# A graph layer's row gathers: two units in 60 fetched row by row from the queues of SyncE and ScalarE

## The chip, the core and the metric

The kernel runs on one core of a Trainium2 chip. A core has TensorE (PE in the profile; PEld is its loading of weights), VectorE (DVE), ScalarE (ACT), GpSimd (POOL) and SyncE (SP). They run side by side, each through its own instructions in order, and wait for each other through semaphores. SP, ACT and POOL can each start DMAs. The metric is the time of one execution on the device, in microseconds.

## What is computed

There are 50,000 nodes with 160 numbers each (64 scalars and 32 vectors of three), and 1,650,000 edges, sorted by their target `dst`. Each edge has four numbers, `sh`. The reference, cut to what matters:

```python
ss, vv = s[src], v[src]                      # 64 scalars, 32 vectors of the source node
e0, e1 = sh[:, 0:1], sh[:, 1:4]
dot = jnp.einsum('eui,ei->eu', vv, e1)
out0 = C0 * (ss * e0 @ W1 + dot * INV3 @ W2)
p3 = (ss @ W3)[:, :, None] * e1[:, None, :] * INV3
p4 = jnp.einsum('eui,uw->ewi', vv * e0[:, :, None], W4) * INV3
p5 = jnp.einsum('eui,uw->ewi', jnp.cross(vv, e1[:, None, :]), W5) * INV6
out1 = C1 * (p3 + p4 + p5)
m_agg = segment_sum(concatenate([out0, out1]), dst, num_segments=n)
h = m_agg's scalars @ Ws * LIN_S, m_agg's vectors by Wv * LIN_V
y = x + (x + relu(h))
out = (y - mean) / sqrt(var + 1e-5)          # over the 160 numbers of a node
```

All of it is linear in the source row times one of four edge numbers. The kernel therefore sums those products by target first and applies the weights, folded into one matrix for each edge number, after the sum. What is left for each edge is to fetch a row of 640 bytes.

## The kernel before

**Tiles.** A *unit* is 128 edges, one on each partition. Six units (`G`) make a *group*, whose edges have targets within a window of 32 nodes (`W`). Two groups (`PG`) make a *pair* of 12 units, and 20 groups (`SG`) a *section* of 120 units. There are 2,149 groups, 1,075 pairs and 108 sections, all written out by Python loops.

**Loading a section.** `load` (L186) runs one section ahead. SP fetches the section's source and target indices (`ri`) and edge numbers (`ra`), 120 units by 128. ACT casts the indices to `rf`, PE transposes them so that a unit becomes a column, and DVE casts the sources back to integers (`si`). The edge numbers stay transposed in PSUM as `pk`. `place` (L208) subtracts each group's first target (`rel`).

**A pair.** `group_sums` (L219) has POOL issue one indirect DMA for each unit (L225). It takes 128 row addresses from a column of `si` and writes 128 rows of `x` into `xg`, of which pool `rowp` has eight buffers. DVE compares targets with slot numbers (`hot`, L230) and multiplies by the four edge numbers (`ha`, L233). For each unit PE multiplies `ha` with `xg` (L238) into `ps` (two buffers), and ACT copies `ps` to `A` (L241).

**Two pairs.** `apply_weights` (L244) transposes `A` on PE (`pt`, L253), copies it on ACT to two tiles `at` (L256), multiplies with the folded weights (`phc`, L263) and copies the result on ACT to `hp` (L267). `block` (L270) sums the windows into blocks of 128 nodes with a 0/1 matrix (`phb`, L286). The node's own rows come by a DMA on SP (`xt`, L275) and are doubled on ACT (`x2`, L277). `norm` (L143) adds and normalizes on DVE, with a square root on ACT (`rstd`, L152), and ACT's queue writes the rows out (L156).

**Order.** The loop calls `group_sums` of a pair before the weights of the two pairs ahead of it. The order on each engine is then made by a scheduler when the program is built. It also deals the DMAs of SP and ACT over eight completion semaphores: a DMA waits until the one that used its semaphore before has landed.

**Later passes.** L358 and on handle indices that don't fit the windows. A flag is loaded into registers (L359). For these inputs their loops run zero times.

Of the kernel before, what the change touches and what calls it, by code (L numbers as in the profile page):

```python
# [29 lines left out]

F32 = mybir.dt.float32
I32 = mybir.dt.int32
AF = mybir.ActivationFunctionType
ALU = mybir.AluOpType
AX = mybir.AxisListType
ET = mybir.EngineType
PSUM = bass.MemoryType.PSUM

P = 128
MUL0, MUL1 = 64, 32  # L40
D = MUL0 + 3 * MUL1
# [10 lines left out]
QG = P // W  # L52
PG = 2
SG = 20


def plan(n_nodes, n_edges):

    nblk = 125
    assert n_nodes % nblk == 0  # L60
    nb = n_nodes // nblk
    again = 9

    per_unit = P * n_nodes / n_edges
    group = max(g for g in range(1, 17)
                if g == 1 or g * per_unit + 1 + 5 * math.sqrt(g * per_unit * per_unit / P) <= W)
    ngroups = math.ceil(math.ceil(n_edges / P) / group)
    units = P * math.ceil(max(math.ceil(n_edges / P) + again - 1, QG * math.ceil(ngroups / QG) * group) / P)
    return nblk, nb, again, group, units, ngroups
# [3 lines left out]
def tile_gnn_resnorm(ctx: ExitStack, tc: tile.TileContext, x, src, dst, attr, W1, W2, W3, W4, W5, Ws, Wv, out, n_edges):  # L73
    nc = tc.nc
    N = x.shape[0]
    NBLK, NB, GA, G, NU, NG = plan(N, n_edges)
# [14 lines left out]
    BWb = const.tile([D - P, NK, D], F32, name="BWb")  # L91
    more = const.tile([1, 2], I32, name="more")

    src1 = src.rearrange("(e o) -> e o", o=1)
    dst1 = dst.rearrange("(e o) -> e o", o=1)

    def weights(wp, psum):
# [45 lines left out]
    def norm(pool, ph, x2, n, row):  # L143
# [7 lines left out]
        rstd = pool.tile([P, 1], F32, name="rstd")  # L151
        nc.scalar.activation(rstd[:n], mv[:n, 1:2], AF.Sqrt, bias=eps_t[:n])  # L152
        nc.vector.reciprocal(rstd[:n], rstd[:n])  # L153
# [15 lines left out]
    alive = max(bs[-1] - bs[0] for bs in of_block) + 1  # L169
    NSC = math.ceil(NG / SG)  # L170

    with tc.tile_pool(name="once", bufs=1) as once, tc.tile_pool(name="raw", bufs=2) as rawp, \
            tc.tile_pool(name="idx", bufs=2) as idxp, tc.tile_pool(name="rows", bufs=8) as rowp, \
            tc.tile_pool(name="ops", bufs=3) as op, tc.tile_pool(name="sums", bufs=4) as sump, \
            tc.tile_pool(name="hp", bufs=alive + 3) as hpp, tc.tile_pool(name="node", bufs=3) as np_, \
            tc.tile_pool(name="psC", bufs=1, space=PSUM) as psC, tc.tile_pool(name="psK", bufs=2, space=PSUM) as psK, \
# [9 lines left out]
        def load(s):  # L186

            n = (min(NG, (s + 1) * SG) - s * SG) * G
            u0 = s * SG * G
            e = slice(u0 * P, (u0 + n) * P)  # L190
            ri = rawp.tile([P, 2, P], I32, name="ri")
            ra = rawp.tile([P, P, NK], F32, name="ra")
            nc.sync.dma_start(ri[:n, 0, :], src1[e].rearrange("(u p) o -> u (p o)", p=P))
            nc.sync.dma_start(ri[:n, 1, :], dst1[e].rearrange("(u p) o -> u (p o)", p=P))
            nc.sync.dma_start(ra[:n].rearrange("u p k -> u (p k)"), attr[e].rearrange("(u p) k -> u (p k)", p=P))
            rf = rawp.tile([P, 2, P], F32, name="rf")
            nc.scalar.copy(rf[:n], ri[:n])
            pi = psI.tile([P, 2, P], F32, name="pi")
            for i in range(2):
                nc.tensor.transpose(pi[:, i, :n], rf[:n, i, :], ident[:n, :n])  # L200
            si = idxp.tile([P, P], I32, name="si")
            nc.vector.tensor_copy(si[:, :n], pi[:, 0, :n])  # L202
            pk = psK.tile([P, NK, P], F32, name="pk")
            for k in range(NK):
                nc.tensor.transpose(pk[:, k, :n], ra[:n, :, k], ident[:n, :n])
            return s, n, si, pi, pk

        def place(loaded):  # L208

            s, n, si, pi, pk = loaded  # L210
            rel = idxp.tile([P, P], F32, name="rel")
            nc.vector.tensor_tensor(
                rel[:, :n].rearrange("p (g j) -> p g j", j=G), pi[:, 1, :n].rearrange("p (g j) -> p g j", j=G),
                baseB[:, s * SG:s * SG + n // G].unsqueeze(2).to_broadcast([P, n // G, G]), op=ALU.subtract)
            nc.vector.tensor_reduce(extremes[:, 0, s:s + 1], rel[:, :n], axis=AX.X, op=ALU.min)
            nc.vector.tensor_reduce(extremes[:, 1, s:s + 1], rel[:, :n], axis=AX.X, op=ALU.max)
            return si, rel, pk

        def group_sums(placed, u, ng):  # L219

            si, rel, pk = placed
            n = ng * G
            xg = rowp.tile([P, PG * G, D], F32, name="xg")
            for j in range(n):
                nc.gpsimd.indirect_dma_start(  # L225
                    out=xg[:, j, :], out_offset=None, in_=x,
                    in_offset=bass.IndirectOffsetOnAxis(ap=si[:, u + j:u + j + 1], axis=0))

            hot = op.tile([P, PG * G, W], F32, name="hot")
            nc.vector.tensor_tensor(hot[:, :n], slotsP[:, 0:W].unsqueeze(1).to_broadcast([P, n, W]),  # L230
                                    rel[:, u:u + n].unsqueeze(2).to_broadcast([P, n, W]), op=ALU.is_equal)
            ha = op.tile([P, PG * G, NK, W], F32, name="ha")
            nc.vector.tensor_tensor(ha[:, :n], hot[:, :n].unsqueeze(2).to_broadcast([P, n, NK, W]),  # L233
                                    pk[:, :, u:u + n].rearrange("p k u -> p u k").unsqueeze(3)
                                    .to_broadcast([P, n, NK, W]), op=ALU.mult)
            ps = psA.tile([P, PG, D], F32, name="ps")
            for j in range(n):
                nc.tensor.matmul(ps[:, j // G, :], ha[:, j].rearrange("p k w -> p (k w)"), xg[:, j, :],  # L238
                                 start=j % G == 0, stop=j % G == G - 1)
            A = sump.tile([P, PG, D], F32, name="A")  # L240
            nc.scalar.copy(A[:, :ng], ps[:, :ng])  # L241
            return A, ng

        def apply_weights(pairs):  # L244
# [3 lines left out]
            for f0, f1 in ((0, P), (P, D)):  # L248
                pt = psM.tile([P, QG, P], F32, name="pt", tag="misc")
                g = 0  # L250
                for A, n in pairs:
                    for i in range(n):
                        nc.tensor.transpose(pt[:f1 - f0, g, :], A[:, i, f0:f1], ident)  # L253
                        g += 1
# [15 lines left out]
        def block(b, hps):  # L270
# [15 lines left out]
                nc.tensor.matmul(ph[:nb], hot2[:r, i, :nb], hp[:r], start=i == 0, stop=i == len(cs) - 1)  # L286
            norm(np_, ph[:nb], x2[:nb], nb, row)

        loaded = {0: load(0)}


        base_d = dram.tile([NGP, 1], I32, name="base_d")
        with nc.allow_non_contiguous_dma(reason="one number of each group"):
            nc.sync.dma_start(base_d, dst1[0:NGP * G * P].rearrange("(g e) o -> g (e o)", e=G * P)[:, 0:1])
        baseI = once.tile([P, NGP], I32, name="baseI")
        nc.sync.dma_start(baseI, base_d.rearrange("g o -> o g").to_broadcast([P, NGP]))
# [3 lines left out]
        for g in range(QG):  # L300
            r = slice(g * W, (g + 1) * W)
# [4 lines left out]
        placed = {0: place(loaded.pop(0))}  # L306
# [10 lines left out]
        g = 0  # L317
        while g < NG:
            s = g // SG
            if g % SG == 0 and s + 1 < NSC:  # L320
                loaded[s + 1] = load(s + 1)
            ng = min(PG, NG - g, (s + 1) * SG - g)
            got = group_sums(placed[s], (g - s * SG) * G, ng)
            if ready:
                second(*ready.pop())
            pairs.append(got)
            g += ng
            if g % QG == 0 or g == NG:
                ready.append((c, pairs))
                pairs, c = [], c + 1  # L330
            if g % SG == 0 and g < NG:
                placed[s + 1] = place(loaded.pop(s + 1))
                del placed[s]
# [3 lines left out]
        far = once.tile([P, NCH], F32, name="far")  # L337
# [25 lines left out]
    mm_d = dram.tile([2, NU], F32, name="mm_d")  # L363
    tab_d = dram.tile([2, NB], I32, name="tab_d")
    tab = const.tile([1, 2, NB], I32, name="tab")
# [7 lines left out]
    with tc.tile_pool(name="up", bufs=1) as up, tc.tile_pool(name="us", bufs=2) as us, tc.For_i(0, once_more, 1):  # L373
# [16 lines left out]
        far = up.tile([PB, 2, CB, nseg], F32, name="far2")  # L390
        for s in range(nseg):
# [7 lines left out]
            for c in range(CB):  # L399
# [3 lines left out]
                at = us.tile([PB, 2, SEG], F32, name="at")  # L403
# [5 lines left out]
        f = up.tile([PB, CB], F32, name="f")  # L409
# [12 lines left out]
    with tc.tile_pool(name="edges2", bufs=2) as ep, tc.tile_pool(name="ops2", bufs=2) as op, \  # L422
# [3 lines left out]
        with tc.For_i(0, blocks, 1) as b:  # L426
# [5 lines left out]
            with tc.For_i(u0, u1, GA) as u:  # L432
                u = nc.s_assert_within(u, 0, NU - GA, skip_runtime_bounds_check_because="below u1")
# [9 lines left out]
                xg = op.tile([P, GA, D], F32, name="xg2")  # L443
# [10 lines left out]
                ps = psA.tile([NBLK, 2, 512], F32, name="ps2")  # L454
# [7 lines left out]
            for f0, f1 in ((0, P), (P, D)):  # L462
# [3 lines left out]
                at = np_.tile([f1 - f0, NK, NBLK], F32, name=f"ac{f0}")  # L466
# [3 lines left out]
            i = 0  # L470
# [4 lines left out]
            row = ds(b * NBLK, NBLK)  # L475
# [37 lines left out]
```

## Time and profile before

Median 16161.78 us of three runs (16160.94 to 16164.18). The profiled execution took 16161.21 us, with a span of 16159.5.

| engine | busy us | share of the span | instructions |
|---|---|---|---|
| PE | 13061.2 | 81% | 43943 |
| PEld | 9172.6 | 57% | 43944 |
| DVE | 3450.3 | 21% | 5361 |
| ACT | 1521.6 | 9% | 3583 |
| POOL | 12192.5 | 75% | 12905 |

Matmuls are pipelined and their ends are modelled, so 81% is not PE at its peak. The granted clock of TensorE is 0.662 of full speed. Instructions that issue a DMA on SP or ACT, load registers or wait are not counted as busy. The core's 16 DMA engines are busy between two and three tenths of the time, and move 72 GB/s.

| queue | packets | MB | share of 16 engines |
|---|---|---|---|
| POOL's (q0) | 618912 | 1057.10 | 26.6% |
| q1 | 102084 | 72.77 | 1.6% |
| q10 | 56864 | 32.58 | 0.7% |

In lines of groups the numbers after the bar are busy time, mean nanoseconds of one, idle time of the engine just before, and what ended most of it. "issue" is idle time in which the engine waited for nothing that the profile shows. In lines of a timeline the first two numbers are start and duration; "SPq" and "ACTq" are the queues' own instructions, and several in one line are merged. Lines of one source line give least, median and greatest duration in nanoseconds. Lines of DMA issues give size and median time from issue to landing.

### The profile page before, as it was taken

How to read it: one execution, taken by the hardware profiler on the slowest of the kernel's cores; microseconds unless marked ns; L12 is line 12 of the kernel's file. 1: busy time of each engine (PE TensorE's matmuls, PEld its weight loads, DVE VectorE, ACT ScalarE, POOL GpSimd, SP SyncE). 2: the span in 40 equal slices, each digit the busy share in tenths (PEclk: the TensorE clock that was granted, in tenths of full speed). 3: DMA queues.
4: the chain of work that ended last, by engine and by line, in shares of the span. 5: the costliest groups of instructions: out<-in, count | busy, mean ns of one | idle time of the engine just before them, and what ended most of it. 6: DMA issues, size and time to landing. Idle time of an engine off the chain costs nothing. (4 is left out here: it accounts for less than half of the span.)

```text
span 16159.5 us, 115933 instructions
## 1 busy us (share of the span) xinstructions
PE 13061.2 (81%) x43943; PEld 9172.6 (57%) x43944; DVE 3450.3 (21%) x5361; ACT 1521.6 (9%) x3583; POOL 12192.5 (75%) x12905
## 2 busy tenths in 40 slices
PE   7878888878888887888888888888788888887887
PEld 5555555555555555555555555555555555555555
DVE  2222222222222222222222222222222222222221
ACT  1000000000000000000000000000000000000000
POOL 7777777777777777777777777777777777777776
PEclk6666666666666666666666666666666666666666
DMA  3222222222222222222222222222222222222222
GB/s 79 73 72 72 73 73 72 72 73 72 72 73 72 72 73 73 72 73 72 73 72 73 72 73 72 73 72 72 73 72 73 72 72 72 73 73 72 72 71 65
DMA packets 778423, 1169.89 MB, mean 72 GB/s; under 512 B 226314, under 2 KB 558406, under 8 KB 777732
## 3 DMA queue, kind: packets, MB, share of 16 engines
q0 software_dynamic: 618912, 1057.10, 26.6%
q1 hardware_dynamic: 102084, 72.77, 1.6%
q10 hardware_dynamic: 56864, 32.58, 0.7%
q8 instruction: 346, 5.67, 0.1%
q14 instruction: 217, 1.78, 0.0%
HBM read 1129.30 MB, written 32.25 MB: 72 GB/s over the span
## 5 line engine op out<-in xcount | busy, mean ns | idle before, releaser
L225 POOL DMA_INDIRECT xg<-in_x,si x12894 | 12190.9, 945 | 3933.3 <-issue 3793.9
L238 PE MATMUL ps<-xg,ha 128*128 128x160 f32 x25788 | 8965.8, 457 | 3056.3 <-DMA xg<-in_x,si 2998.2
L238 PEld LDWEIGHTS ps<-xg,ha 128*128 128x128 f32 x25788 | 5534.5, 267 | 6130.7 <-DMA xg<-in_x,si 5458.9
L233 DVE TENSOR_TENSOR ha<-hot,pk 128x1536 f32<-128x1536 f32 x1075 | 1884.7, 1753 | 10801.5 <-PE ps L238 10801.5
L263 PE MATMUL phc<-BWb,at 32*128 32x160 f32 x4304 | 1624.9, 471 | 0.0
L241 ACT COPY A<-ps 128x320 f32<-128x320 f32 x1075 | 456.8, 425 | 11583.8 <-PE ps L238 11569.5
L253 PE MATMUL pt<-ident,A 128*128 128x128 f32 x4298 | 1361.4, 394 | 0.4 <-ACT at L256 0.4
L286 PE MATMUL phb<-hp,hot 128*128 128x160 f32 x4584 | 1349.4, 483 | 0.0
L286 PEld LDWEIGHTS phb<-hp,hot 128*128 128x128 f32 x4584 | 1202.2, 331 | 129.0 <-issue 129.0
L263 PE MATMUL phc<-BWa,at 128*128 128x160 f32 x4304 | 1262.7, 386 | 0.0
L263 PEld LDWEIGHTS phc<-BWb,at 32*128 32x128 f32 x4304 | 892.6, 256 | 557.2 <-issue 556.7
L263 PEld LDWEIGHTS phc<-BWa,at 128*128 128x128 f32 x4304 | 1026.0, 270 | 0.4 <-DVE st L148 0.2
L253 PEld LDWEIGHTS pt<-ident,A 128*128 128x128 f32 x4298 | 750.1, 175 | 104.8 <-ACT at L256 0.8
L256 ACT COPY at<-pt 128x512 f32<-128x512 f32 (+1 forms) x1076 | 623.2, 579 | 1137.6 <-PE pt L253 1137.4
L230 DVE TENSOR_TENSOR hot<-slotsP,rel 128x384 f32<-128x384 f32 x1075 | 597.0, 556 | 31.4
L281 DVE TENSOR_TENSOR hot<-slotsP,rr 128x768 f32<-128x768 f32 (+2 forms) x391 | 362.9, 928 | 0.0
L146 DVE SCALAR_TENSOR_TENSOR y<-phb,x 128x160 f32<-128x160 f32 x391 | 126.9, 325 | 800.3 <-PE phb L286 800.3
L277 ACT ACTIVATE x<-xt 128x160 f32<-128x160 f32 x391 | 131.6, 337 | 1341.7 <-DVE y L146 1341.2
L202 DVE CAST si<-pi 128x120 int32<-128x120 f32 x108 | 30.4, 282 | 882.9 <-DMA xg<-in_x,si 879.7
L267 ACT COPY hp<-phc 128x160 f32<-128x160 f32 x538 | 157.3, 292 | 195.0 <-PE phc L263 194.9
L155 DVE TENSOR_SCALAR o<-y,mv,rstd 128x160 f32<-128x160 f32 x391 | 149.2, 382 | 14.1
L152 ACT ACTIVATE rstd<-mv,eps_t 128x1 f32<-128x1 f32 x391 | 115.2, 295 | 334.3 <-DVE mv L150 329.6
(67 smaller groups left out, 856.0 us busy)
## 6 DMA issues: line engine op xcount, KB each, us to landing
xg<-in_x,si POOLq DMA_INDIRECT x12894, 2.6
xt<-in_x SPq DMA_DIRECT2D x390, 80.0 KB, 1.9
out<-o ACTq DMA_DIRECT2D x390, 80.0 KB, 1.7
ra<-in_attr SPq DMA_DIRECT2D x107, 240.0 KB, 3.0
ri<-in_src SPq DMA_DIRECT2D x107, 60.0 KB, 2.0
ri<-in_dst SPq DMA_DIRECT2D x107, 60.0 KB, 2.0
baseI<-base_d SPq DMA_DIRECT2D x1, 1076.0 KB, 7.5
BVd<-BV ACTq DMA_DIRECT2D x1, 240.0 KB
```

The source lines that it names most:

```text
L155: nc.vector.tensor_scalar(o[:n], y[:n], mv[:n, 0:1], rstd[:n], op0=ALU.subtract, op1=ALU.mult)
L225: nc.gpsimd.indirect_dma_start(out=xg[:, j, :], out_offset=None, in_=x, in_offset=bass.IndirectOffsetOnAxis(ap=si[:, u + j:u + j + 1], axi ...
L230: nc.vector.tensor_tensor(hot[:, :n], slotsP[:, 0:W].unsqueeze(1).to_broadcast([P, n, W]), rel[:, u:u + n].unsqueeze(2).to_broadcast([P, n ...
L233: nc.vector.tensor_tensor(ha[:, :n], hot[:, :n].unsqueeze(2).to_broadcast([P, n, NK, W]), pk[:, :, u:u + n].rearrange("p k u -> p u k").un ...
L238: nc.tensor.matmul(ps[:, j // G, :], ha[:, j].rearrange("p k w -> p (k w)"), xg[:, j, :], start=j % G == 0, stop=j % G == G - 1)
L241: nc.scalar.copy(A[:, :ng], ps[:, :ng])
L253: nc.tensor.transpose(pt[:f1 - f0, g, :], A[:, i, f0:f1], ident)
L256: nc.scalar.copy(at[:, :, :ng].rearrange("f k g w -> f g k w"), pt[:f1 - f0, :ng].rearrange("f g (k w) -> f g k w", w=W))
L263: nc.tensor.matmul(ph[:ng * W], at[:, k, :ng].rearrange("f g w -> f (g w)"), bw[:, k, :], start=i == 0, stop=i == 2 * NK - 1)
L267: nc.scalar.copy(hp[:ng * W], ph[:ng * W])
L281: nc.vector.tensor_tensor(hot2[:, :len(cs)], slotsP.unsqueeze(1).to_broadcast([P, len(cs), P]), rr[:, :len(cs)].unsqueeze(2).to_broadcast( ...
L286: nc.tensor.matmul(ph[:nb], hot2[:r, i, :nb], hp[:r], start=i == 0, stop=i == len(cs) - 1)
```

## The change

In each section four of the 120 units are no longer gathered by POOL. They are the last units of pairs 4 and 9 (SP's queue) and of pairs 2 and 7 (ACT's), counted from 0. For each such unit the queue's engine loads 128 row offsets into registers, 32 at a time, and starts one DMA of 640 bytes for each row. The 32 rows of a step belong to one pair: the steps are spread over the four pairs ahead of the one that needs the unit. In the source a step stands behind the pair's matmuls and ahead of the copy to `A`. ACT multiplies the source indices by 640 into `ro` to make byte offsets. The fetched unit has a tile of its own, `xr`, in a pool with three buffers for each queue, and the unit's matmul reads it.

```diff
+HELP = {ET.SP: (4, 9), ET.Activation: (2, 7)}
+ROWS = 32
...
+    xbytes = x.bitcast(U8).rearrange("n f -> (n f)")
...
+            tc.tile_pool(name="far", bufs=3) as farp, \
...
+            ro = rawp.tile([P, P], I32, name="ro")
+            nc.scalar.mul(ro[:n], ri[:n, 0, :], 4.0 * D)
+            offsets[s] = ro
...
-        def group_sums(placed, u, ng):
+        def group_sums(placed, u, ng, q):
...
-            for j in range(n):
+            xr = fetched.pop(q, None)
+            for j in range(n - (xr is not None)):
                 nc.gpsimd.indirect_dma_start(
                     out=xg[:, j, :], out_offset=None, in_=x,
...
-                nc.tensor.matmul(ps[:, j // G, :], ha[:, j].rearrange("p k w -> p (k w)"), xg[:, j, :],
+                nc.tensor.matmul(ps[:, j // G, :], ha[:, j].rearrange("p k w -> p (k w)"),
+                                 xr if xr is not None and j == n - 1 else xg[:, j, :],
                                  start=j % G == 0, stop=j % G == G - 1)
+            for eng in HELP:
+                fetch(q, eng)
             A = sump.tile([P, PG, D], F32, name="A")
             nc.scalar.copy(A[:, :ng], ps[:, :ng])
...
+        queues = {ET.SP: nc.sync, ET.Activation: nc.scalar}
+        offsets, fetched = {}, {}
+        ppair = SG // PG
+        steps = P // ROWS
+        todo = {}
+        for s in range(NSC):
+            for eng, at in HELP.items():
+                for m in at:
+                    q = s * ppair + m
+                    if q >= steps and (s * SG + (m + 1) * PG) <= NG:
+                        for i in range(steps):
+                            todo.setdefault((q - steps + i, eng), []).append((q, s, (m + 1) * PG * G - 1, i))
+
+        def fetch(q, eng):
+
+            for q1, s, u, i in todo.pop((q, eng), []):
+                if i == 0:
+                    fetched[q1] = farp.tile([P, D], F32, name=f"xr{list(HELP).index(eng)}")
+                xr = fetched[q1]
+                _, at = nc.values_load_multi_w_load_instructions(
+                    offsets[s][u:u + 1, i * ROWS:(i + 1) * ROWS], engines=[eng], min_val=0, max_val=(N - 1) * 4 * D,
+                    skip_runtime_bounds_check_because="an offset of a row of x")
+                for j, v in enumerate(at):
+                    r = i * ROWS + j
+                    queues[eng].dma_start(xr[r:r + 1, :].bitcast(U8),
+                                          xbytes[ds(v, 4 * D)].rearrange("(o f) -> o f", o=1))
...
-            got = group_sums(placed[s], (g - s * SG) * G, ng)
+            got = group_sums(placed[s], (g - s * SG) * G, ng, s * ppair + (g - s * SG) // PG)
```

In the built program 428 gathers are gone from POOL. SP and ACT have 27,392 more DMAs each and 856 loads of 32 registers each, and ACT has 108 more multiplications.

More of the change, by code (lines that the diff above doesn't have):

```diff
@@ L32 @@
 I32 = mybir.dt.int32
+U8 = mybir.dt.uint8
 AF = mybir.ActivationFunctionType
```

## The prediction, made before the result was known

> **What bounds the kernel now.** I read the page's slices first (every engine is equally busy from start to end, so one stretch stands for all), then the groups of instructions, the waits, and the timelines of POOL, ACT and SP. Groups:
>
> ```profile
> L225 POOL DMA_INDIRECT xg<-in_x,si x12894 | 12190.9, 945 | 3933.3 <-issue 3793.9
> L238 PE MATMUL ps<-xg,ha 128*128 128x160 f32 x25788 | 8965.8, 457 | 3056.3 <-DMA xg<-in_x,si 2998.2
> L241 ACT COPY A<-ps 128x320 f32<-128x320 f32 x1075 | 456.8, 425 | 11583.8 <-PE ps L238 11569.5
> ```
>
> POOL is busy 12190.9 us and idle 3933.3, nearly all of it "issue": it waits for nobody. Both add up to 16124.2, the span of 16159.5 less start and tail. PE waits for gathers, ACT for PE. POOL's timeline shows the beat:
>
> ```profile
> 8.93 0.95 POOL L225 DMA_INDIRECT xg<-in_x,si  x1 [0.30 <-issue]
> 10.18 0.95 POOL L225 DMA_INDIRECT xg<-in_x,si  x1 [0.30 <-issue]
> ...
> 16125.51 0.94 POOL L225 DMA_INDIRECT xg<-in_x,si  x1 [0.30 <-issue]
> ```
>
> One gather each 0.95 + 0.30 = 1.25 us, first at 7.5, last done at 16126.5: 12,894 x 1.25 = 16,118. So gather issue on POOL is the bound; start and tail are about 40 us. A section of 120 units takes 150.0 us, a pair of 12 units 15.0. In the table by stretches a section gives ACT 14 us of work and PE 121 to 124 (at a clock of 0.64 to 0.67). PE's share is paced by gathers: where many are there already it does 58 of these matmuls in 10.61 us, so it has room.
>
> What the new work will use, the queues of SP and ACT:
>
> ```profile
> 8010.86 29.74 SPq L275 DMA_DIRECT2D xt<-in_x  x2
> 8072.35 0.35 SPq L195 DMA_DIRECT2D ra<-in_attr  x1
> 8100.77 0.33 SPq L275 DMA_DIRECT2D xt<-in_x  x1
> 8115.53 0.35 SPq L193 DMA_DIRECT2D ri<-in_src  x1
> 8115.93 0.40 SPq L194 DMA_DIRECT2D ri<-in_dst  x1
> 8132.48 0.35 SPq L275 DMA_DIRECT2D xt<-in_x  x1
> ```
> ```profile
> L359 SPq TENSOR_LOAD <-more x2: 290/382/475, 16144.6 to 16148.4; - x2
> L359 ACTq TENSOR_LOAD <-more x2: 293/390/487, 16145.5 to 16151.0; - x2
> ```
> ```profile
> xt<-in_x SPq DMA_DIRECT2D x390, 80.0 KB, 1.9
> out<-o ACTq DMA_DIRECT2D x390, 80.0 KB, 1.7
> ```
>
> One DMA occupies its queue 0.33 to 0.35 us; two in a row start 0.40 apart and the second takes 0.40. From issue to landing is 1.7 to 1.9 us. Loading one register takes 0.29 to 0.49.
>
> **What the Trainium skill says.** "DMA: Bandwidth & Descriptors", section "Issuing engines are not separate DMA queues": starting DMAs from several engines saves only the sequencer's time, usually small beside the transfer. Here that time is what POOL lacks; but "usually small" does not hold for one row. The same page, "Anatomy of one DMA", gives about 2.0 us fixed for a DMA, mostly the wait until the last byte is confirmed, and about 50 ns of dispatch. The landing (1.7 to 1.9) agrees; the queue's 0.33 to 0.40 is far above 50 ns, and the trace decides. For a register load, "Latency and other measured facts" gives a floor of about 600 ns (the trace has 290 to 487 for one), and "Runtime: NRT & Kernel Launch", section "Instruction fetch mechanics", about 200 ns for each register even in bulk, there for loads from HBM. No run here shows 32 at once.
>
> **The change part by part.**
>
> 1. Gathers removed. 12,894 - 428 = 12,466 (each queue takes two units in each of 107 sections' worth: 214). 428 x 1.25 = -535 us, if POOL remains the bound: 16161.2 - 535 = 15,626 against the profiled execution, which lies 0.6 us under the median shown. A section then takes 116 x 1.25 = 145.0 us.
>
> 2. Row DMAs added. 214 x 128 = 27,392 on each queue, 256 in a section. In the built program each waits for the DMA that last used its completion semaphore. There are eight, dealt over both queues; where both fetch, a queue gets one back at every fourth of its own DMAs (over half of all; most others five to eight; a fifth wait for one of the other queue). With 1.7 us to land and about 0.1 to notice, four in flight give 1.8 / 4 = 0.45 us each. Bounds: 0.35 (one DMA's queue time, nothing waits) and 0.50 (1.9 us landing). I take 0.45: 32 rows cost 14.4 us (11.2 to 16). That is by itself a pair's 14.5 us.
>
> 3. Register loads added: 856 on each queue, of 32 registers. Below: 0.4 us (a load of one, if more cost nothing). Above: 32 x 0.2 = 6.4 (the page's price, an estimate). I take 2.0: one address after the other must cost something, and SBUF, not HBM, is read. A step of 32 rows is then 16.4 us.
>
> 4. Offsets scaled on ACT: 108 more instructions like the cast beside them (0.40), 43 us in all, beside POOL's work. The matmul that reads xr in place of xg costs the same, but adds a wait: PE stops there until the unit's rows have landed, and behind it stand all of PE's later matmuls and so A, at and xg's buffers. On ACT that unit's last rows stand ahead of the copy A of the pair before, so they have landed by then unless the queue itself is late, which is step 6.
>
> 5. What stands behind the fetches on ACT. ACT runs in order; in the built program a step's 32 DMAs lie between two copies A<-ps. Behind them wait A, hence PE's transposes, then the copies at, the weight matmuls, hp and the block's matmuls. SP has only its few loads behind them, needed tens of us later. ACT's other work of a section is 14 us busy, four output DMAs (1.2), and waits that used to vanish in 11.6 ms of idleness but now stand between fetches: the timeline shows A to at 1.3 us, at to at 0.6, and before hp about 1.6 (sixteen weight matmuls take some 2.6 at full pace, partly under at). 3.5 us every second pair is 17.5 a section. Sum: 32.8.
>
> 6. Sum for ACT alone: eight steps, 8 x 16.4 + 32.8 = 164 us a section, against POOL's 145. 107.5 sections x 164 + 40 = 17,670.
>
> 7. The two queues together. Since the completion semaphores are dealt in one order over both, neither can run more than about eight DMAs ahead of the other. Of ten steps six have both queues fetching, two SP alone, two ACT alone. If that lock is complete, ACT cannot fetch while SP does its own step: 10 x 16.4 + 0.8 x 32.8 = 190 us, and 107.5 x 190 + 40 = 20,465. Only a fifth of the waits cross, so I take the middle of 17,670 and 20,465: about 19,050.
>
> 8. Buffers and DMA engines. rowp's eight buffers smooth over eight pairs (120 us), but a mean rate above 145 us a section uses them up within a few sections; then POOL waits for PE to free xg. DMA engines are not the limit: q0 uses 26.6% and all queues under 30; even 32 packets a row, 1.75 million, at q10's mean of 32 ns (0.7% of 16 engines over 56,864 packets) add 22%.
>
> **The rivals.**
>
> A. POOL stays the bound, faster. If 32 rows and their registers together cost under (145 - 32.8) / 8 = 14.0 us, ACT fits, and with a full lock the limit is (145 - 26.2) / 10 = 11.9. That needs rows at 0.35 to 0.40 and a register load under 1 us. For it: a queue time of 0.33 to 0.35, a row of 640 bytes may land sooner than 80 KB, and the eight buffers of slack. Against it: 0.40 already at two DMAs in a row, and landing that is not known to shrink. Time: 15,626. Chance 0.20.
>
> B. Register loads decide, much slower. At 0.2 us a register a load takes 6.4 us; a step is 20.8: 8 x 20.8 + 32.8 = 199 for ACT alone, 10 x 20.8 + 26.2 = 234 locked; 21,430 to 25,200, the middle about 23,300. For it: the page's price. Against it: it is given for HBM, and one register from SBUF costs 0.29. Chance 0.11.
>
> C. ACT and POOL near balance, about 16,160, within 0.2%: needs 150 us a section by chance. 0.03.
>
> Forecast, 0.66: ACT's queue, with SP's tied to it, is the bound; 16,200 to 22,000 with its bounds (a step of 12.5 to 19 us).
>
> **How the numbers follow.** A measurement of this kernel tells about 0.2% (32 us) from no change. Faster 0.20 (A), same 0.03 (C), slower 0.77 (forecast and B). Predicted 19,050. The range goes down to A, since leaving both A and B out would leave out over 2 in 10: 15,600 to 22,000. The forecast's own range is 16,200 to 22,000.
>
> **What would show it.** POOL's beat stays 1.25 us, but its idle time is no longer "issue": gathers wait for PE ps. ACT's group A<-ps no longer shows 11.6 ms idle for PE. PE idles for ACT (A, at) and for row DMAs. On the queues, row DMAs start 0.40 to 0.50 us apart, with waits named after DMAs; register loads take 1 to 3 us. A section takes 164 to 190 us. The forecast is wrong if POOL's idle is still all "issue" (A), if rows start every 0.35 us with no wait for landing, or if register loads take over 5 us (B). If PE's busy share falls while ACT's queue has gaps without any wait, I have missed a mechanism.

## The result, and the profile after

The changed kernel takes 17678.03 us, median of four runs (17649.97 to 17694.64), beside 16161.47 for the kernel before: a ratio of 1.0936 (95% interval 1.0917 to 1.0955), 1,517 us slower. The profiled execution took 17694.64, with a span of 17692.9. Groups of the page, as before:

```profile
L236 POOL DMA_INDIRECT xg<-in_x,si x12466 | 11784.8, 945 | 5772.5 <-issue 3683.7
L249 PE MATMUL ps<-xg,ha 128*128 128x160 f32 x24932 | 4848.1, 359 | 3969.4 <-ACT A L255 3945.7
...
L267 PE MATMUL pt<-ident,A 128*128 128x128 f32 (+1 forms) x4298 | 928.6, 338 | 4569.3 <-ACT A L255 4369.6
...
L255 ACT COPY A<-ps 128x320 f32<-128x320 f32 x1075 | 457.7, 426 | 11169.1 <-DMA xr<-in_x 10587.2
```

A gather still takes 945 ns, and 428 fewer of them stand in the list. But POOL's idle time rose from 3933.3 to 5772.5 us, and "issue" no longer fills it. PE, which waited for gathers before, now waits for ACT's copy `A`, 8.3 ms in two groups. ACT's copy in turn no longer waits for PE but behind the row DMAs. The list of waits (engine and line, what it waited for, us in total, times, longest) has the same waits and adds what POOL's new idle time stands for:

```profile
ACT A L255 <- DMA xr<-in_x: 10587.2, 841, 18.4
...
POOL xg L236 <- PE ps L249: 1163.3, 303, 8.5
POOL xg L236 <- PE phb L300: 896.0, 161, 10.1
```

Page and list together: POOL waits for PE to free buffers of `xg`, PE waits for ACT, ACT for its row DMAs. The prediction named this chain. ACT's timeline over two pairs shows how it looks (start, duration, what, and in brackets the engine's idle time before, in which the queue's own instructions count as idle):

```profile
8031.28 0.43 ACT L255 COPY A<-ps 128x320 f32<-128x320 f32 x1 [8.79 <-DMA xr<-in_x]
8033.74 13.31 ACTq L328 DMA_DIRECT2D xr<-in_x  x32
8047.14 0.43 ACT L255 COPY A<-ps 128x320 f32<-128x320 f32 x1 [15.44 <-DMA xr<-in_x]
8047.47 1.05 ACT L270 COPY at<-pt 128x512 f32<-128x512 f32 x2
8053.12 0.29 ACT L281 COPY hp<-phc 128x160 f32<-128x160 f32 x1 [4.60 <-PE phc L277]
8055.48 11.53 ACTq L328 DMA_DIRECT2D xr<-in_x  x32
8067.05 0.43 ACT L255 COPY A<-ps 128x320 f32<-128x320 f32 x1 [13.64 <-DMA xr<-in_x]
```

And PE in the same stretch:

```profile
8032.66 4.64 PE L249 MATMUL ps<-xg,ha 128*128 128x160 f32 x24
8047.62 0.90 PE L249 MATMUL ps<-xg,ha 128*128 128x160 f32 x2 [10.31 <-ACT A L255]
8048.32 2.34 PE L277 MATMUL phc<-BWa,at 128*128 128x160 f32 x8
8050.59 2.49 PE L277 MATMUL phc<-BWb,at 32*128 32x160 f32 x8
```

PE does a pair's matmuls in 4.64 us and stands for 10.31 until ACT has issued its 32 rows and copied `A`. Then ACT stands for 4.60, because `hp` needs the weight matmuls. Neither engine is full; they take turns.

The queues' own instructions (least, median and greatest duration in ns):

```profile
L328 SPq MOVE xr<-in_x x27392: 29/29/38, 20.0 to 17449.9; - x200
L328 SPq DMA_DIRECT2D xr<-in_x x27392: 227/228/379, 20.1 to 17450.0; - x200
L328 ACTq MOVE xr<-in_x x27392: 29/29/38, 31.5 to 17652.9; - x200
L328 ACTq DMA_DIRECT2D xr<-in_x x27392: 234/234/564, 31.6 to 17652.9; - x200
```
```profile
L323 SPq TENSOR_LOAD <-ro x856: 2095/2176/2460, 17.8 to 17427.4; - x172
L323 ACTq TENSOR_LOAD <-ro x856: 2108/2200/2717, 28.7 to 17640.1; - x172
```

A row is a register move and a DMA, 0.26 us of queue time, and a load of 32 registers takes 2.2 us. I added up ACT's whole stream of records, giving each instruction its time beyond the end of the one before and the gap ahead of it:

| on ACT | ms | us a section (of 107.5) |
|---|---|---|
| rows: DMA and move themselves | 7.32 | 68.1 |
| rows: gaps ahead of them (semaphores, start) | 3.49 | 32.4 |
| register loads, where not beside a copy | 1.59 | 14.8 |
| gaps ahead of hp | 2.04 | 18.9 |
| gaps ahead of rstd | 1.13 | 10.5 |
| gaps ahead of A | 0.55 | 5.1 |
| everything else (copies, output DMAs, small gaps) | 1.57 | 14.6 |
| sum | 17.69 | 164.6 |

### The profile page after: what moved, and what is told of

The parts are those of the page before. It is cut to its first block, busy times and chain, and to the rows that moved or that the text cites. A ratio compares the mean times of both kernels' runs of the same rounds, so it can differ in the third digit from the quotient of the medians.

```text
span 17692.9 us, 227783 instructions
## 1 busy us (share of the span) xinstructions
PE 8753.2 (49%) x43943; PEld 8060.0 (46%) x43944; DVE 3437.6 (19%) x5361; ACT 1394.4 (8%) x3691; POOL 11786.3 (67%) x12477
## 5 line engine op out<-in xcount | busy, mean ns | idle before, releaser
L236 POOL DMA_INDIRECT xg<-in_x,si x12466 | 11784.8, 945 | 5772.5 <-issue 3683.7
L249 PE MATMUL ps<-xg,ha 128*128 128x160 f32 x24932 | 4848.1, 359 | 3969.4 <-ACT A L255 3945.7
L249 PEld LDWEIGHTS ps<-xg,ha 128*128 128x128 f32 x24932 | 4557.3, 240 | 4147.1 <-ACT A L255 4049.5
L267 PE MATMUL pt<-ident,A 128*128 128x128 f32 (+1 forms) x4298 | 928.6, 338 | 4569.3 <-ACT A L255 4369.6
L267 PEld LDWEIGHTS pt<-ident,A 128*128 128x128 f32 (+1 forms) x4298 | 533.3, 143 | 4770.7 <-ACT A L255 4479.0
L277 PE MATMUL phc<-BWb,at 32*128 32x160 f32 x4304 | 1063.5, 406 | 0.0
L300 PE MATMUL phb<-hp,hot 128*128 128x160 f32 x4584 | 1033.1, 379 | 0.0
L300 PEld LDWEIGHTS phb<-hp,hot 128*128 128x128 f32 x4584 | 876.4, 246 | 97.2 <-issue 96.9
L270 ACT COPY at<-pt 128x512 f32<-128x512 f32 (+1 forms) x1076 | 565.4, 581 | 73.0 <-DMA xr<-in_x 51.9
L249 PE MATMUL ps<-xr,ha 128*128 128x160 f32 x856 | 250.7, 384 | 171.2 <-DMA xr<-in_x 135.2
L249 PEld LDWEIGHTS ps<-xr,ha 128*128 128x128 f32 x856 | 188.4, 254 | 184.7 <-DMA xr<-in_x 135.3
```

Source lines behind the costliest of these rows:

```text
L236: nc.gpsimd.indirect_dma_start(out=xg[:, j, :], out_offset=None, in_=x, in_offset=bass.IndirectOffsetOnAxis(ap=si[:, u + j:u + j + 1], axi ...
L270: nc.scalar.copy(at[:, :, :ng].rearrange("f k g w -> f g k w"), pt[:f1 - f0, :ng].rearrange("f g (k w) -> f g k w", w=W))
L277: nc.tensor.matmul(ph[:ng * W], at[:, k, :ng].rearrange("f g w -> f (g w)"), bw[:, k, :], start=i == 0, stop=i == 2 * NK - 1)
```

## The experiments

The theory to test: ACT's queue works in order, and rows, register loads, copies and waits together take 164 us a section where POOL needs 145. The rivals: the rows themselves are slow wherever they are issued; the completion semaphores that both queues share hold them up; the order around `A` is at fault, not the sum. Where not said otherwise, a kernel below is the changed one with the edit shown.

**Each queue alone.**

```diff
-HELP = {ET.SP: (4, 9), ET.Activation: (2, 7)}
+HELP = {ET.SP: (4, 9)}
```

> Only SP's two units of a section are fetched row by row; ACT's two go back to POOL. Theory 'ACT's queue' (fetching in front of the copies on ACT is what stretches a section to 164 us): nothing stands before the copies any more, POOL is the bound again with 214 gathers fewer: 16161 - 214 x 1.25 = 15,894 us. Rival 'row fetching itself' (tiny DMAs, the wait of PE for a fetched unit, or the order that the scheduler made cost PE or POOL time wherever they are issued): not below 16,161, about 16,900 if half of the loss is SP's.

Measured: 15901.41 us, ratio 0.9839 (0.9823 to 0.9855). The theory's number, 15,894, is met within 8 us; the rival of slow rows falls. Two groups of its page:

```profile
L236 POOL DMA_INDIRECT xg<-in_x,si x12680 | 11991.5, 946 | 3873.3 <-issue 3732.8
...
L249 PE MATMUL ps<-xr,ha 128*128 128x160 f32 x428 | 186.6, 540 | 5144.1 <-DMA xr<-in_x 3847.1
```

POOL waits for nobody again. Yet PE waits 3.8 ms for fetched rows: that is idle time of an engine that is not the bound, and `rowp`'s eight buffers hide it.

```diff
-HELP = {ET.SP: (4, 9), ET.Activation: (2, 7)}
+HELP = {ET.Activation: (2, 7)}
```

> Only ACT's two units of a section are fetched row by row; SP's two go back to POOL. All eight completion semaphores then turn on ACT's DMAs, so a row waits for the eighth before it and not the fourth. Theory 'shared semaphores' (waits of rows for semaphores, 3.5 ms on ACT's queue, are what makes it late): rows start every 0.27 us instead of 0.38, a section on ACT falls from 164 to about 135 us, POOL is the bound: 15,894. Rival 'ACT alone' (issue, register loads and waits for PE fill ACT whatever SP does, the pace is that of landing): 17,400 to 17,700.

Measured: 16529.94 us, ratio 1.0229 (1.0202 to 1.0255). Neither side's number. ACT issues alone, so that a row mostly needs the semaphore of the eighth before it. Of its 27,392 rows 104 stand until that semaphore is free (they start within 60 ns of the landing, after a gap); in the changed kernel 8,725 did. The time falls by 1,150 us: rows and their gaps take 88.2 us a section on ACT and not 100.6. But 153.6 us a section remain, over POOL's 147.5. Shared semaphores are a part of the loss; without them ACT alone is still too slow. The timeline shows steps at an even pace, with the same waits for PE between them:

```profile
8033.38 0.43 ACT L255 COPY A<-ps 128x320 f32<-128x320 f32 x1 [12.32 <-DMA xr<-in_x]
8033.70 1.05 ACT L270 COPY at<-pt 128x512 f32<-128x512 f32 x2
8039.36 0.29 ACT L281 COPY hp<-phc 128x160 f32<-128x160 f32 x1 [4.61 <-PE phc L277]
8041.65 11.07 ACTq L328 DMA_DIRECT2D xr<-in_x  x32
```

**The copies taken off ACT.** `A`, `at`, `hp` and `x2` are made by DVE.

```diff
-            nc.scalar.copy(A[:, :ng], ps[:, :ng])
+            nc.vector.tensor_copy(A[:, :ng], ps[:, :ng])
...
-            nc.scalar.copy(hp[:ng * W], ph[:ng * W])
+            nc.vector.tensor_copy(hp[:ng * W], ph[:ng * W])
```

> Both queues fetch as in the changed kernel, but the copies A, at, hp and x2 are made by DVE. Theory 'ACT's queue' (what costs is that PE's copies stand behind 32 row DMAs): PE no longer waits for ACT, ACT has 116 us of fetching a section and some waits, POOL is the bound: about 15,630 to 15,800. Rival 'the queues cannot fetch fast enough' (rows arrive late because of landing, register loads and the lock between the two queues): PE waits for xr, 17,000 or more.

Measured: 16185.99 us, ratio 1.0016 (1.0008 to 1.0024). Of the 2,052 us between the changed kernel and the 15,626 of a free POOL, 1,492 are gone; 560 stay. What stays is a ring that I had not seen:

```profile
ACT rstd L157 <- DVE mv L155: 10774.6, 309, 72.2
DVE x L291 <- DMA xt<-in_x: 6796.8, 296, 47.2
PE ps L249 <- DMA xr<-in_x: 6272.0, 158, 51.9
```

PE now waits for rows, up to 51.9 us. ACT's rows stand behind `rstd`. During most of those 10.8 ms ACT's queue issues rows, but for 1.2 ms it stands still ahead of `rstd`, and 1.18 of these fall in blocks whose `x2` (`x` in the trace, now made by DVE) came later than their sums. `x2` waits for the node's own rows `xt`. SP's queue issues `xt` behind rows, and SP's rows wait 2.1 ms for semaphores that ACT's rows hold: the ring is closed. One instruction that waits is enough to hold a queue. In the changed kernel a late `x2` holds ACT's queue for only 5 us, so this ring came with the edit; how much of the 560 us it makes is not shown.

**The register loads taken out.** The row DMAs get fixed addresses, rows worked out when the program is built; the indexed rows are not fetched for these units.

```diff
-                _, at = nc.values_load_multi_w_load_instructions(
...
-                for j, v in enumerate(at):
+                for j in range(ROWS):
                     r = i * ROWS + j
+                    v = ((q1 * 1021 + r * 389) % N) * 4 * D
...
-                                          xbytes[ds(v, 4 * D)].rearrange("(o f) -> o f", o=1))
+                                          xbytes[v:v + 4 * D].rearrange("(o f) -> o f", o=1))
```

> The row DMAs have fixed addresses (rows worked out when the program is built, not the indexed ones), so the register loads and moves are gone and nothing else. If ACT's queue is serial, 8 x 2.2 us of loads and 256 x 0.03 of moves go from a section on ACT: 164 - 25 = 139, under POOL's 145: 15,630 to 15,900. If the loads lie beside work that ACT waits for anyway (copies run on ACT's engine while its queue loads registers, and PE waits follow), less than half of it comes back: 16,500 to 17,200. If the DMAs' own pace is all that counts: 17,600.

Measured: 15635.23 us, ratio 0.9674 (0.9658 to 0.9690). As many DMAs, both queues, the same place in the source, and POOL is the bound, 9 us from the 15,626 that part 1 of the prediction worked out:

```profile
L236 POOL DMA_INDIRECT xg<-in_x,si x12466 | 11787.2, 946 | 3810.5 <-issue 3616.0
```

Loads and moves are 25 us of queue time a section, and ACT lacked almost 20. The rows did not become quicker: they start mostly 0.27 to 0.55 us apart, and with their gaps they take 110 us a section on ACT where they took 100.6, 17 of them in waits for semaphores that SP's rows hold. That does no harm while ACT keeps up with POOL. The place of the fetches and the lock between the queues are in this kernel too; neither is a cause by itself.

**Less for ACT, and another order.** One unit for ACT and not two:

```diff
-HELP = {ET.SP: (4, 9), ET.Activation: (2, 7)}
+HELP = {ET.SP: (4, 9), ET.Activation: (6,)}
```

> SP fetches its two units of a section, ACT one (the last of pair 6) and not two; the fourth goes back to POOL. Theory 'ACT's sum' (rows, register loads, copies and waits of a section have to fit ACT's queue): four steps of about 14 us and 48 us of the rest give some 104 us, well under 146; POOL is the bound with 321 gathers fewer: 16161 - 321 x 1.25 = 15,760 us. Rival 'any fetch in front of the copies makes PE and ACT wait for each other', and rival 'lock between the queues': more than the kernel with SP's units alone (15,901), 16,000 to 16,900.

The fetches behind the copy to `A`:

```diff
-            for eng in HELP:
-                fetch(q, eng)
             A = sump.tile([P, PG, D], F32, name="A")
             nc.scalar.copy(A[:, :ng], ps[:, :ng])
+            for eng in HELP:
+                fetch(q, eng)
```

> The changed kernel with a step's fetches written behind the copy to A and not in front of it; in the built program 32 row DMAs then stand between A and the copies at. Theory 'ACT's sum': ACT's rows, loads and copies are the same, only which wait stands behind them changes: 17,300 to 17,900. Rival 'the place in front of A': PE gets its copies in time, the waits for PE vanish from ACT, 15,630 to 16,500.

These two took 25926.60 and 23930.28 us, but the kernel before took 18380.33 beside them, so the absolute numbers answer nothing. The same happened once more (e7_sp_two_act_one 25877.40, e8_fetch_behind_A 23793.41, e9_sp_three 27727.08, the kernel before 18401.20). What the traces show of it stands under the last heading. The same three kernels beside a kernel before at its usual time:

> SP's two units and one of ACT's, a third time, to see it beside a kernel before that takes 16,161 us. Theory 'ACT's sum': ACT has some 104 us of work and waits in a section, POOL is the bound with 321 gathers fewer, 15,760 us. Rival 'lock between the queues' (rows of one queue wait for semaphores of the other, and copies behind them): 16,000 to 16,900.

Measured: 15805.27 us, the kernel before 16204.54, ratio 0.9755 (0.9738 to 0.9771). The theory's ratio is 15,760 / 16,161 = 0.975. POOL's idle time is nearly all "issue" again:

```profile
L236 POOL DMA_INDIRECT xg<-in_x,si x12573 | 11923.7, 948 | 3843.8 <-issue 3721.0
```

Rows, moves, loads and their gaps take 55 us a section on ACT, and POOL is the bound with three quarters of the gathers gone that the changed kernel took off it. This version is the best of those tried that compute everything: faster than the kernel before and, by its ratio, 11% faster than the changed one.

> The changed kernel with a step's fetches written behind the copy to A, beside a kernel before at its usual time. Theory 'ACT's sum': the same work on ACT in another order, 1.08 to 1.11 times the time before. Rival 'the place in front of A': PE gets its copies in time and POOL becomes the bound again, 0.967 to 1.02.

Measured: 17800.08 us, ratio 1.1009 (1.0991 to 1.1028), as the sum has it. The wait moved from `A` to `at`:

```profile
ACT at L270 <- DMA xr<-in_x: 7257.6, 531, 26.8
...
PE phc L277 <- ACT at L270: 4794.2, 526, 19.4
```

Either way most of a step's 32 rows stand in one piece ahead of a copy. An order in which rows fill ACT's waits ahead of `A`, `hp` and `rstd` was not tried. These waits are 34.5 us of the section's 164.6; by the table's sum ACT's work would fit under POOL's 145 without them.

**Three units for SP, none for ACT.**

```diff
-HELP = {ET.SP: (4, 9), ET.Activation: (2, 7)}
+HELP = {ET.SP: (2, 5, 8)}
```

> Three units of a section on SP's queue, none on ACT's, beside a kernel before at its usual time. Theory 'a queue's sum': rows 384 x 0.323 and loads 12 x 2.18 make 150 us a section, over the 146.2 of 117 gathers, and waits for output DMAs come on top: 1.00 to 1.15 times the time before. Rival 'SP's queue costs nothing': POOL is the bound, 0.975.

Measured: 18897.62 us, ratio 1.1693 (1.1673 to 1.1712), slower than the theory's range. Waits of SP's queue, and of DVE and PE:

```profile
SPq L328 <- DMA out<-o: 2088.2, 387, 39.5
```
```profile
DVE ha L244 <- PE ps L249: 11101.8, 1071, 38.6
...
PE ps L249 <- DMA xr<-in_x: 8967.6, 318, 42.3
```

The kind of result is the theory's: a queue with 150 us of work of its own where POOL takes 146 becomes the bound, without any copy in it. The size was off because I had put the waits for output DMAs down as mostly slack. They are 2.09 ms, 19 us a section: the row waits for a semaphore that an output DMA holds. In 1.8 of these 2.09 ms the output's block stands on DVE behind `ha`, which waits for PE, and PE waits for rows. Apart from these waits rows take 0.332 us on average (127 us a section), loads 26, and the rest of the queue 4; with the 19 that is the 176 measured.

## Why the prediction was right, step by step

The bound and the direction were right. The number was 1,370 us too high, and part 7 accounts for all of it.

- **What bounds, and the gain (part 1).** Right. Where the queues keep up, the time is the number of gathers times 1.25 us: within 9 us with 428 and with 214 gone.
- **Row DMAs (part 2).** Too dear: 0.45 us was taken, 0.39 measured on ACT, gaps included. The term that was mis-sized is the landing. It was taken from DMAs of 80 KB, 1.7 us and 0.1 to notice. By the semaphore events of the trace one row has landed 1.56 us after its start (median on ACT), and a row that waits for it starts some 0.02 us later; a quarter of that is 0.39. The four-in-flight reading was right in kind, since with eight in flight a row takes 0.35. But 0.39 is a mean: a third of ACT's rows wait for a landing, and two thirds follow at once, 0.33 us apart. Rows every 0.35 us without such a wait had been named as a sign that the forecast is wrong, and they are the majority here. The lower bound of 0.35 was the queue time of a DMA over 128 partitions; one row takes 0.23, and with its move it can start every 0.32 to 0.33 us.
- **Register loads (part 3).** 2.0 us taken, 2.2 measured; close, by luck as much as by reason, since the bounds were 0.4 and 6.4. The upper one came from the Trainium skill's price ("Runtime: NRT & Kernel Launch", section "Instruction fetch mechanics", about 200 ns a register, given there for HBM); from SBUF a register more costs about 60 ns, an estimate from the 2.2 us for 32 and the 0.29 for one.
- **What stands behind the fetches (part 5).** Too cheap: 32.8 us a section (its terms add up to 32.7), 49 measured. The terms of the sum that were mis-sized are the waits. `hp` was given 8 us a section and has 18.9. I priced it at what the weight matmuls take at full pace, but PE often finishes other matmuls of its order first, or runs the weight matmuls at half pace after standing still. `rstd` and `A` were given no wait at all, and have 10.5 and 5.1. The waits ahead of `at`, priced at 9.5, are gone (8 us in the whole run).
- **ACT's sum (part 6).** 164 predicted, 164.6 measured. That close, it is luck: 15 us too many for rows and 16 too few for waits cancel.
- **The two queues together (part 7).** This step failed in size. 1,380 us were added for the lock, and the time came to 17,678, next to the 17,670 of ACT alone. Sharing the semaphores does cost 1,150 us, as ACT's queue alone shows, but that cost lies in part 2, in the four DMAs in flight. What the lock adds on ACT is small: its rows wait 0.2 ms in all for semaphores that SP's rows hold. SP, which has less to do, takes up the waiting: its rows wait 3.7 ms for rows, 2.7 of them for ACT's. The lower end of the forecast, 16,200, needs the lock too: with a step of 12.5 us ACT alone comes to 8 x 12.5 + 32.8 = 132.8 us, under POOL's 145.
- **Packets (part 8).** Up to 32 a row were allowed for. There are two:

```profile
q1 hardware_dynamic: 156868, 90.41, 2.0%
q10 hardware_dynamic: 111648, 50.22, 1.1%
```

Either queue has 54,784 packets more than before, twice 27,392. All queues together keep the DMA engines busy for 25% of the span, so they are not the limit.

- **The rivals.** A needed a step of under 14 us for 32 rows and their load; measured are 14.4 with what is hidden left out, and the rest of ACT's work was larger than A allowed. B fell with loads of 2.2 us.

## What to carry to other kernels

When work is moved from a saturated engine to "idle" queues, add up the receiving engine's whole in-order stream for one period of the bound: queue time of what is added, what it waits for, and the old waits that were free only while the engine had nothing behind them. Under the period the gain was there nearly in full; with 4% over it (ACT alone) or 13.5% (the changed kernel), all of the gain and more was lost. Writing the fetches behind `A` instead of ahead of it did not help; a finer mixing of rows and copies is open. Move as much as fits: here three units of the four, two on SP and one on ACT.

## What the runs showed of the hardware that I had not expected

- A load of 32 registers takes 2.2 us where one takes 0.29 to 0.49. A DMA of one row holds its queue for 0.23 us, where one over 128 partitions takes 0.33 to 0.35.
- PE is slow after standing still. After a wait of ten microseconds and two other matmuls, the first eight weight matmuls (BWa) take 2.34 us in the timeline above. After 6.8 us of matmuls without a pause the same eight take 1.25:

```profile
8012.03 4.99 PE L249 MATMUL ps<-xg,ha 128*128 128x160 f32 x26
8016.85 1.25 PE L277 MATMUL phc<-BWa,at 128*128 128x160 f32 x8
```

In the whole run 411 such groups of eight begin within 1 us of the end of a pause of over 5 us, and take 2.30 to 2.50 us; 104 begin 5 to 8 us after one, and take 1.25.
- In the first tries of the last three kernels single instructions on the queues stalled. Of SP's 27,396 register moves with two units for SP and one for ACT, 4,268 took over 0.1 us, most of those near 0.69, where in the changed kernel's profile the longest takes 0.042. The kernel before lost 14% under this; these kernels took 34 to 64% more than at other times. Both times it was on chips on which none of the other experiments ran. The cause stays open: there is no trace of the kernel before from there.
